# One activation table set for Ln and Exp, adjacent Gelus in each band, and a 3x3 convolution without two matrix blocks, in a four-layer convolution kernel

## The chip, the cores and the metric

The kernel runs on one core of one Trainium2 chip. The metric is the device time of one execution in microseconds (us). The time before is 4928.02 us, the median of three runs that lie between 4917.86 and 4933.94 us. One further execution was taken with the hardware profiler; all durations below come from it.

## What is computed

Four residual layers on x of shape (4, 384, 64, 64), float32, each on a group-normed input. Cut to what matters here:

```
x = x + attention(gn(x))       # layer 0: q,k,v from 96 channels, softmax over 4096 positions, 1x1 projection of 384
x = x + L1(gn(x))              # layer 1: 1x1 conv, 8x8 patch FFT filter, depthwise 3x3, gate, 1x1 conv:
                               #   x1, x2 = halves of the depthwise output (192 channels each); gelu(x1) * x2
x = x + L2(gn(x))              # layer 2: y3 = bn(depthwise 3x3(x)); y5 = bn(depthwise 5x5(x));
                               #   tok = bn(kw0*y3 + kw1*y5 + y1); gates; MLP 384 -> 768 -> 384 with bn and gelu
x = x + L3(gn(x))              # layer 3: depthwise 7x7, its kernel made from channel means and maxima
```

A norm needs 1/sqrt(var + eps). The kernel computes it on ScalarE as exp(-0.5 * ln(var + eps)).

## The kernel before

The program is written with a layer that records instructions, places tiles and orders each engine's queue by a priority heap over its own time estimates[...]. `tc.high_priority()` lifts the instructions of a block in that heap; `tc.issue_after(i)` puts them behind instruction i on i's engine.

**Stage A, 0 to about 2490 us (layers 0 and 1), `phase_a`.** Batches b = 0 to 3 go through `attention` (L739 on), 64 steps each. A step is four score matmuls (`sc_s`, L755, 32 rows each), two Exp activations of 128x1024 on ScalarE (`probs`, L763) and four value matmuls (`av`, L792). Beside the attention of batch b, `others` feeds pieces of other work: the statistics and the q, k, v of batch b+1 (`qkv`, whose `layer_norm` calls `rsqrt`, L354 and L355: one Ln and one Exp for each of eight blocks), and layer 1 of batch b-1. After about 2220 us the last batch's layer 1 runs alone.

Layer 1 works in 8 bands of 8 image rows. For each band `band_taps` (L967 to L997) accumulates nine taps for three tiles acc[0], acc[1], acc[2] on VectorE (L988; in the last batch some taps are matmuls). The channels are ordered so that acc[0] and the lower half of acc[2] are x1, and acc[1] and the upper half of acc[2] are x2. When acc[1] is done (j == 1), acc[0] goes through Gelu (L992) and is multiplied into acc[1] (L993); when acc[2] is done (j == 2), its lower half goes through Gelu into acc[0]'s upper half (L995), which is multiplied into acc[2] (L996). `band_out` (L1005, L1006) does the 1x1 convolution of the result some tiles later.

Ln, Exp and Gelu are table functions: where an activation's function is not in the active table set, the compiler puts an ACT_TABLE_LOAD ahead of it, which carries the line of that activation. Nothing in the kernel before chooses a set.

**Stage B, about 2490 to 3090 us (layer 2's depthwise convolutions), `phase_b`.** 12 units of 32 channels (four batches side by side on the partitions). A unit has 16 steps n, each for two channels. A step multiplies strips of the image (`z_`) with banded matrices (`toep`), which VectorE (even n) or GpSimd (odd n) makes from a row of taps and a band mask, one instruction of 128x1536 (`matrices53`, L1177). The taps come by DMA, a tile of 384 KB for four steps (`taps53`, L1163). `conv53` (L1196) runs, for each channel, three matmuls i of 256 columns over rows of the strip two apart: 128 columns for the 5x5 filter (v = 0), 128 for the 3x3 filter (v = 1), all into one bank `conv_m`. One ScalarE copy of 512 moves the bank into `d_o` (L1205), VectorE takes two statistics (L1208), and after each four steps two DMAs of 512 KB store d (L1211, ScalarE's queue). At a unit's end `conv_norms` makes its scales with one Ln and one Exp; in the next unit `unit_tok` reads d back (L1261, SyncE's queue, three buffers), combines it on ScalarE and VectorE (L1269, L1272, L1274, L1279) and stores tok (L1282). `unit_strips` loads and transposes a later unit's image (L1110, L1124).

**Stages E, F and G, 3125 to 4920 us:** layer 2's MLP (`phase_ef`: `h_s`, L1420; `h_m`, L1472) and layer 3 (`phase_g`: `conv_m`, L1786). There the change touches only which table set is active at a few places.

## Time and profile before

| | us |
|---|---|
| median of three runs | 4928.02 |
| the profiled execution's own time | 4921.93 |
| its span, first to last instruction | 4920.2 |
| PE busy | 4484.3 |
| DVE busy | 2787.8 |
| ACT busy | 2155.9 |
| POOL busy | 777.6 |

PE is TensorE's matmuls, PEld its weight loads, DVE is VectorE, ACT is ScalarE, POOL is GpSimd. Busy time is the union of an engine's instructions. A float32 matmul stands in the trace as two records, so counts of matmuls are twice those of the program. A group of instructions has a line, an engine, an operation and its tiles; behind its busy time stands the mean duration of one in ns and the time that the engine sat idle before them, with what ended it. The table loads have no tile.

### The profile page before, as it was taken

To read this page: it belongs to the slowest core of one execution; us is meant where nothing else is said; L and a number is where in the kernel's file an instruction comes from. 1 tells how busy PE (TensorE), PEld (TensorE's weight loads), DVE (VectorE), ACT (ScalarE), POOL (GpSimd) and SP (SyncE) were. 2 spreads that over 40 slices of the span, in tenths; PEclk is the share of its full clock that TensorE was granted. 3 is DMA by queue.
4 is the path that set the end of the run, shared out by engine and by line. 5 is a ranking of instruction groups with operands and counts; after the bars stand their busy time and mean duration, and the time that the engine had idled before them with its cause. 6 is when DMAs were issued, how large, how long until landed. Compare 5 with 4: busy or idle time off the path is not lost.

```text
span 4920.2 us, 47066 instructions
## 1 busy us (share of the span) xinstructions
PE 4484.3 (91%) x17289; PEld 2510.4 (51%) x17289; DVE 2787.8 (57%) x4506; ACT 2155.9 (44%) x2905; POOL 777.6 (16%) x593
## 2 busy tenths in 40 slices
PE   5999999999999999999978999699999997678988
PEld 2333444334443344435467888344444443577888
DVE  5322566645656345565867778555521113667898
ACT  5444444555445544445245666311123334753321
POOL 1000000000000000000035555000000001225554
PEclk9999999999999999999989999799999998788999
DMA  5210211111122111113259999776664444896776
GB/s 176 69 46 28 92 58 60 61 60 47 56 70 67 47 33 65 65 62 112 83 169 282 288 295 299 250 270 254 250 240 153 154 152 143 309 343 195 234 252 229
DMA packets 345844, 752.21 MB, mean 153 GB/s; under 512 B 22683, under 2 KB 172294, under 8 KB 336646
## 3 DMA queue, kind: packets, MB, share of 16 engines
q1 hardware_dynamic: 279864, 475.07, 31.4%
q0 software_dynamic: 32640, 151.28, 7.9%
q10 hardware_dynamic: 33102, 122.77, 6.4%
q8 instruction: 140, 2.29, 0.2%
q14 instruction: 98, 0.80, 0.1%
HBM read 446.76 MB, written 302.25 MB: 152 GB/s over the span
## 4 chain that ended last, share of the span: by engine, by line
PE 67%; DVE 13%; ACT 8%; DMA 7%; issue 4%; POOL 1%; SPq 0%; ACTq 0%; DVEq 0%; POOLq 0%
PE av L792 14%; PE h_s L1420 10%; PE h_m L1472 9%; PE conv_m L1196 9%; PE sc_s L755 5%; PE proj_m L825 4%; PE t_m L911 3%; DVE acc L988 3%; PE out_m L1006 2%; PE conv_m L1786 2%; PE out_m L1005 2%; PE back_m L936 2%; DMA wmix<-in_mix_t 1%; ACT probs L763 1%; DMA g_h<-h 1%
## 5 line engine op out<-in xcount | busy, mean ns | idle before, releaser
L792 PE MATMUL av<-probs,vt 128*128 128x512 f32 x2048 | 964.6, 606 | 0.1
L763 ACT ACTIVATE probs<-sc_s 128x1024 f32<-128x1024 f32 x512 | 501.1, 1021 | 721.3 <-PE av L792 717.9
L792 PEld LDWEIGHTS av<-probs,vt 128*128 128x128 f32 x2048 | 369.7, 192 | 467.9 <-issue 460.5
L1196 PE MATMUL conv_m<-toep,z 128*128 128x256 f32 x2304 | 520.1, 385 | 10.3 <-DVE toep L1177 6.4
L988 DVE SCALAR_TENSOR_TENSOR acc<-band,vecs,acc 128x512 f32<-128x512 f32 x708 | 496.6, 746 | 45.7 <-POOL band L949 40.0
L1472 PE MATMUL h_m<-f_h,cm_w_t 128*128 128x512 f32 x1152 | 496.6, 594 | 8.8 <-ACT f_h L1462 8.7
L1196 PEld LDWEIGHTS conv_m<-toep,z 128*128 128x128 f32 x2304 | 439.0, 193 | 71.7 <-DVE z L1129 4.9
L1786 PE MATMUL conv_m<-toep,z 128*128 128x128 f32 x3072 | 391.4, 285 | 40.5 <-POOL toep L1773 21.6
L1786 PEld LDWEIGHTS conv_m<-toep,z 128*128 128x128 f32 x3072 | 377.0, 201 | 42.8 <-POOL toep L1773 22.0
L1177 POOL TENSOR_TENSOR toep<-w,band 128x1536 f32<-128x1536 f32 x94 | 323.8, 3445 | 281.7 <-PE conv_m L1196 240.8
L1420 PE MATMUL h_s<-e_tok,cm_w_t 128*128 128x512 f32 x768 | 362.6, 594 | 5.5 <-DMA e_tok<-tok 5.5
L1472 PEld LDWEIGHTS h_m<-f_h,cm_w_t 128*128 128x128 f32 x1152 | 219.3, 191 | 286.1 <-issue 273.5
L755 PE MATMUL sc_s<-q,k 32*128 32x512 f32 x2048 | 296.5, 648 | 25.7 <-ACT probs L763 25.2
L1480 DVE BATCH_NORM_STATS2 h_st<-f_h 128x6 f32<-128x512 f32 x96 | 66.4, 694 | 429.2 <-ACT f_h L1479 429.2
L911 PE MATMUL t_m<-w_in_t,xb 128*128 128x384 f32 x768 | 276.4, 494 | 4.7 <-DVE coef L928 3.5
L825 PE MATMUL proj_m<-xm,w_proj_t 128*128 128x512 f32 x576 | 269.4, 606 | 9.4 <-DVE xm L778 6.5
L1427 ACT COPY e_h<-h_s 128x1024 f32<-128x1024 f32 x96 | 97.2, 1012 | 400.8 <-PE h_s L1420 400.8
L832 DVE SCALAR_TENSOR_TENSOR x_res<-proj_m,bn_c,x_res 128x512 f32<-128x512 f32 x96 | 71.7, 747 | 308.7 <-PE proj_m L825 308.7
L1420 PEld LDWEIGHTS h_s<-e_tok,cm_w_t 128*128 128x128 f32 x768 | 146.5, 191 | 189.7 <-issue 183.6
L1429 DVE BATCH_NORM_STATS2 h_st<-e_h 128x6 f32<-128x512 f32 x192 | 123.5, 685 | 199.5 <-ACT e_h L1427 199.5
L911 PEld LDWEIGHTS t_m<-w_in_t,xb 128*128 128x128 f32 x768 | 142.3, 191 | 141.0 <-issue 58.0
L1420 PE MATMUL h_s<-z,cm_w_t 128*128 128x512 f32 x384 | 196.1, 592 | 0.0
(392 smaller groups left out, 6119.3 us busy)
## 6 DMA issues: line engine op xcount, KB each, us to landing
d<-d_o ACTq DMA_DIRECT2D x96, 512.0 KB
c_d<-d SPq DMA_DIRECT2D x96, 512.0 KB
hid<-e_h ACTq DMA_DIRECT2D x16, 3072.0 KB
f_h<-hid SPq DMA_DIRECT2D x16, 3072.0 KB
x_in<-in_x SPq DMA_DIRECT2D x96, 256.0 KB
x_res<-in_x SPq DMA_DIRECT2D x32, 768.0 KB
xa<-x_res POOLq DMA_DIRECT2D x32, 768.0 KB, 3.9
xa_in<-xa SPq DMA_DIRECT2D x32, 768.0 KB
```

Of the source, the lines that this page charges most:

```text
L755: nc.tensor.matmul(s[:, g], lhsT=k4[32 * g : 32 * g + 32, c], rhs=q[i][32 * g : 32 * g + 32], start=True, stop=True,)
L763: nc.scalar.activation(p[:, h * 1024 : (h + 1) * 1024], s[:, 2 * h : 2 * h + 2].rearrange("p a b -> p (a b)"), AF.Exp, scale=0.25,)
L792: nc.tensor.matmul(av, lhsT=vt[:, 4 * c + v, :], rhs=p[:, v * 512 : (v + 1) * 512], start=c == 0 and v == 0, stop=c == 7 and v == 3,)
L825: nc.tensor.matmul(m, lhsT=self.w_proj[:, j, o * P : (o + 1) * P], rhs=xm[:, j], start=j == 0, stop=j == NJ - 1,)
L911: nc.tensor.matmul(m[:, 0:C], lhsT=xb[:, j], rhs=self.w_in[:, j, :], start=j == 0, stop=j == NJ - 1,)
L988: nc.vector.scalar_tensor_tensor(out, src(j, k), w, done, ALU.mult, ALU.add)
L1177: eng.tensor_tensor(t, self.w53[:, at : at + 192].rearrange("p (m n) -> p m n", n=8).unsqueeze(2).to_broadcast([P, 24, 8, 8]), band.rearra ...
L1196: nc.tensor.matmul(m[:, c * 256 : (c + 1) * 256], lhsT=self.z_[:, at : at + P], rhs=t[:, 12 * c + 4 * i : 12 * c + 4 * i + 4].rearrange("p ...
L1420: nc.tensor.matmul(s[:, v, :], lhsT=w1[:, j, o * P : (o + 1) * P], rhs=t[j][:, v * 512 : (v + 1) * 512], start=j == 0, stop=j == NJ - 1,)
L1429: nc.vector.bn_stats(st[:, o, 8 * b + 2 * i + v, :], h[:, o, v * 512 : (v + 1) * 512])
L1472: nc.tensor.matmul(m, lhsT=w2[:, o, j * P : (j + 1) * P], rhs=h[:, o, v * 512 : (v + 1) * 512], start=o == 0, stop=o == 5,)
L1786: nc.tensor.matmul(m[:, ch * P : (ch + 1) * P], lhsT=self.z_[:, at : at + P], rhs=t[:, 8 * c + 2 * i : 8 * c + 2 * i + 2].rearrange("p m a ...
```

## The change

1. `ln_exp` loads the set natural_log_exp_and_others, in which both Ln and Exp lie. It is called at the start, and behind each use of another function (Gelu, Sigmoid, Sqrt) on ScalarE.
2. In `band_taps` both Gelus of a band move to j == 2 and stand next to each other with high priority: first that of acc[2]'s lower half, into a tile of its own (`gelu`, one buffer), then that of acc[0], then `ln_exp`; both multiplications follow.
3. In layer 2 each group of 8 rows of a filter's matrix is a block of 64 columns. `_pair` orders a channel's blocks so that the two blocks of the 3x3 filter that its taps don't reach are left out: 10 blocks for a channel in place of 12. The middle matmul (i = 1) goes first with 256 columns, i = 0 and i = 2 have 192 and write the bank's first and last 192 columns. The matrices and taps shrink from 24 to 20 blocks a step (128x1280 and 320 KB), and the copy out of the bank becomes two copies of 256 (5x5: the middle 128 columns of each channel; 3x3: its first and last 64).
4. In `nets` the two Sigmoids for k3 and k5 stand ahead of those of the gate.

```diff
 def _pair(u, v):
-    return np.stack([u, v], axis=4)
+    u, v = (t.reshape(*t.shape[:4], 2, 8) for t in (u, v))
+    blocks = [
+        (v, 0, 0), (u, 0, 0), (u, 0, 1),
+        (v, 1, 0), (u, 1, 0), (u, 1, 1), (v, 1, 1),
+        (u, 2, 0), (u, 2, 1), (v, 2, 1),
+    ]
+    return np.ascontiguousarray(np.stack([t[:, :, :, k, f] for t, k, f in blocks], axis=3))
...
+    def ln_exp(self, behind=None):
+        load = lambda: self.nc.scalar.preload_act_table_set("natural_log_exp_and_others")
+        if behind is None:
+            load()
+        else:
+            with self.tc.high_priority(), self.tc.issue_after(behind.ins):
+                load()
...
-            if j == 1:
-                nc.scalar.activation(acc[0], acc[0], AF.Gelu)
+            if j == 2:
+                g = self.wk("gelu", "gelu", 1)
+                with self.tc.high_priority():
+                    first = nc.scalar.activation(g[64:P], acc[2][0:64], AF.Gelu)
+                    with self.tc.issue_after(first.ins):
+                        last = nc.scalar.activation(acc[0], acc[0], AF.Gelu)
+                    self.ln_exp(last)
                 nc.vector.tensor_mul(acc[1], acc[1], acc[0])
-            if j == 2:
-                nc.scalar.activation(acc[0][64:P], acc[2][0:64], AF.Gelu)
-                nc.vector.tensor_mul(acc[2][64:P], acc[2][64:P], acc[0][64:P])
+                nc.vector.tensor_mul(acc[2][64:P], acc[2][64:P], g[64:P])
...
-        t = self.bt_p.tile([P, 24, 8, 8], F32, tag="toep", name="toep53", bufs=4)
-        at = n % 4 * 192
+        t = self.bt_p.tile([P, 20, 8, 8], F32, tag="toep", name="toep53", bufs=4)
+        at = n % 4 * 160
...
-            for i in range(3):
+            for i, k0, k1, to in ((1, 3, 7, 0), (0, 0, 3, 0), (2, 7, 10, 64)):
                 at = (c0 + c) * 132 + 4 * i
                 nc.tensor.matmul(
-                    m[:, c * 256 : (c + 1) * 256],
+                    m[:, c * 256 + to : c * 256 + to + 64 * (k1 - k0)],
                     lhsT=self.z_[:, at : at + P],
-                    rhs=t[:, 12 * c + 4 * i : 12 * c + 4 * i + 4].rearrange("p m a n -> p (m a n)"),
-                    start=i == 0,
+                    rhs=t[:, 10 * c + k0 : 10 * c + k1].rearrange("p m a n -> p (m a n)"),
+                    start=i == 1,
                     stop=i == 2,
                 )
-        mv = m.rearrange("p (c v n) -> p v c n", c=2, v=2)
+        mv = m.rearrange("p (c n) -> p c n", c=2)
         at = 2 * (n % 4)
-        nc.scalar.copy(self.d_o[:, :, at : at + 2], mv)
+        nc.scalar.copy(self.d_o[:, 0, at : at + 2], mv[:, :, 64:192])
+        ends = mv.rearrange("p c (k n) -> p c k n", n=64)[:, :, 0:4:3]
+        nc.scalar.copy(self.d_o[:, 1, at : at + 2].rearrange("p c (f n) -> p c f n", f=2), ends)
...
```

`ln_exp` is also called without an argument at the start of `phase_a` and behind `score_shifts`, and behind: the activation in `bn_of_four`, the last Sigmoid of the gate in `nets`, the gates' Sigmoids and the last Gelu of the MLP in `phase_ef`, and the Sqrt in `phase_g`.

More of the change, by code (lines that the diff above doesn't have):

```diff
@@ L392, in bn_of_four @@
         a, c = self.bn_scale_shift(name, mv[:, 0:1], mv[:, 1:2], g, b)
-        nc.scalar.activation(out, z, func, bias=c, scale=a)
+        self.ln_exp(nc.scalar.activation(out, z, func, bias=c, scale=a))
     def of_groups(self, name, v):
@@ L490, in phase_a @@
             self.open_psum(ctx, 2)
+            self.ln_exp()
             cp = ctx.enter_context(tc.tile_pool(name="a_const", bufs=1))
@@ L512, in phase_a @@
             self.score_shifts(cp)
+            self.ln_exp()
             self.w_proj = self.weight(cp, "w_proj_t")
@@ L1160, in taps53 @@
         if n < 16 * UNITS:
-            self.w53_ahead = self.bt_p.tile([P, 8 * 96], F32, tag="w53", name="w53")
+            self.w53_ahead = self.bt_p.tile([P, 8 * 80], F32, tag="w53", name="w53")
             src = self.ins["c53_t"][n // 64][:, n % 64 * 2 : n % 64 * 2 + 8]
-            self.nc.sync.dma_start(self.w53_ahead, src.rearrange("p c t n v -> p (c t n v)"))
+            self.nc.sync.dma_start(self.w53_ahead, src.rearrange("p c m n -> p (c m n)"))
     def matrices53(self, n):
@@ L1178, in matrices53 @@
             t,
-            self.w53[:, at : at + 192].rearrange("p (m n) -> p m n", n=8).unsqueeze(2).to_broadcast([P, 24, 8, 8]),
-            band.rearrange("p (a n) -> p a n", n=8).unsqueeze(1).to_broadcast([P, 24, 8, 8]),
+            self.w53[:, at : at + 160].rearrange("p (m n) -> p m n", n=8).unsqueeze(2).to_broadcast([P, 20, 8, 8]),
+            band.rearrange("p (a n) -> p a n", n=8).unsqueeze(1).to_broadcast([P, 20, 8, 8]),
             ALU.mult,
@@ L1320, in nets @@
         nc.tensor.matmul(m[:, B : 2 * B], lhsT=net[:, P : 2 * P], rhs=z2, start=True, stop=True)
-        self.gate = self.keep.tile([P, B], F32, tag="gate", name="gate")
-        nc.scalar.activation(self.gate, m[:, 0:B], AF.Sigmoid)
-        nc.vector.tensor_scalar(self.gate, self.gate, 0.5, None, ALU.subtract)
-        nc.scalar.activation(self.gate, self.gate, AF.Sigmoid)
         self.k3 = self.keep.tile([P, B], F32, tag="k3", name="k3")
@@ L1328, in nets @@
         nc.scalar.activation(self.k5, m[:, B : 2 * B], AF.Sigmoid, scale=-1.0)
+        self.gate = self.keep.tile([P, B], F32, tag="gate", name="gate")
+        nc.scalar.activation(self.gate, m[:, 0:B], AF.Sigmoid)
+        nc.vector.tensor_scalar(self.gate, self.gate, 0.5, None, ALU.subtract)
+        self.ln_exp(nc.scalar.activation(self.gate, self.gate, AF.Sigmoid))
         own = self.sm([P, B], "k_own")
@@ L1378, in phase_ef @@
                 gates = self.sm([P, B], "gates")
-                nc.scalar.activation(gates, z[:, j], AF.Sigmoid, bias=gc[:, j : j + 1], scale=ga[:, j : j + 1])
+                last = nc.scalar.activation(
+                    gates, z[:, j], AF.Sigmoid, bias=gc[:, j : j + 1], scale=ga[:, j : j + 1]
+                )
                 nc.vector.tensor_scalar(self.at[:, j, :], gates, a[:, j : j + 1], None, ALU.mult)
                 nc.vector.tensor_scalar(self.ct[:, j, :], gates, c[:, j : j + 1], None, ALU.mult)
+            self.ln_exp(last)
             stay = self.sm([P, B], "stay")
@@ L1461, in phase_ef @@
                     for o in range(6):
-                        nc.scalar.activation(
+                        last = nc.scalar.activation(
                             h[:, o, :], h[:, o, :], AF.Gelu, bias=c1[:, o : o + 1], scale=a1[:, o : o + 1]
                         )
+                    if b == B - 1 and i == 3:
+                        self.ln_exp(last)
                     if b == B - 1 and 0 < i:
@@ L1531, in phase_g @@
             nc.vector.tensor_reduce(self.mix2, sq, AX.X, ALU.add)
-            nc.scalar.activation(self.mix2, self.mix2, AF.Sqrt)
+            self.ln_exp(nc.scalar.activation(self.mix2, self.mix2, AF.Sqrt))
             for k in ("a_s", "b_s"):
```

## The prediction

> **What bounds the kernel now.** I read the page first, then the busy time by stage, ScalarE's groups, TensorE's waits, and stage B unit by unit. From the page:

> ```profile
> span 4920.2 us, 47066 instructions
> PE 4484.3 (91%) x17289; PEld 2510.4 (51%) x17289; DVE 2787.8 (57%) x4506; ACT 2155.9 (44%) x2905; POOL 777.6 (16%) x593
> PE   5999999999999999999978999699999997678988
> DMA  5210211111122111113259999776664444896776
> PE 67%; DVE 13%; ACT 8%; DMA 7%; issue 4%; POOL 1%; SPq 0%; ACTq 0%; DVEq 0%; POOLq 0%
> ```

> TensorE carries the kernel nearly everywhere. The one place where a second resource is also full is slices 21 to 25, stage B, where DMA reads 9 beside PE. The stretches by stage (each engine's busy us, granted clock, DMA share, GB/s):

> ```profile
> core 0: us, PE busy (x) PEld busy (x) DVE busy (x) ACT busy (x) POOL busy (x), PEclk, DMA share, GB/s
> 110.00:500.00 390.00, 375.73 (x1215) 149.55 (x1214) 117.73 (x177) 181.79 (x204) 8.44 (x14) 0.97 0.15 49
> 500.00:2220.00 1720.00, 1654.58 (x5423) 714.37 (x5423) 979.19 (x1661) 813.58 (x995) 65.14 (x126) 0.99 0.18 60
> 2490.00:3125.00 635.00, 568.95 (x2720) 492.51 (x2720) 470.45 (x923) 372.53 (x576) 323.81 (x94) 0.95 0.91 272
> ```

> In stage A ScalarE is about half idle and PE has only 65 us of idle time in 1720, so work taken off ScalarE pays only where PE waited for it. The table loads, among ScalarE's groups:

> ```profile
> L354 ACT ACT_TABLE_LOAD x66 | 84.7, 1283 | 21.2 <-POOL mean L1042 9.7 <-PE ln_v L642 4.1 <-DMA vecs<-in_vecs 3.4
> L355 ACT ACT_TABLE_LOAD x56 | 71.8, 1283 | 2.1 <-DMA w_proj_t<-in_w_proj_t 1.2
> L763 ACT ACT_TABLE_LOAD x46 | 59.0, 1283 | 0.8
> L992 ACT ACT_TABLE_LOAD x25 | 32.1, 1283 | 0.5
> L995 ACT ACT_TABLE_LOAD x19 | 24.4, 1283 | 5.7 <-DVE acc L988 5.4
> ```

> With seven single ones that is 219 loads, 281 us of ScalarE. What PE waited for from ScalarE between 500 and 2220 us:

> ```profile
> PE sc_s L755 <- ACT probs L763: 14.2, 22, 2.0
> PE v_m L685 <- ACT ln_rs L354: 9.5, 6, 2.7
> PE back_m L936 <- ACT t_t L919: 5.5, 5, 1.5
> ```

> With two smaller rows (3.2 and 0.8) 33.2 us; the same view of 0 to 500 us has 11.0, 4.2, 2.2 and 1.0, 18.4 us. So 52 us is about all that stage A can give. Stage B by units (1, 2, 5, 6 and 11; a unit starts with its first conv_m matmul):

> ```profile
> 2554.90:2598.60 43.70, 43.70 (x199) 38.34 (x199) 33.64 (x62) 24.18 (x36) 24.15 (x7) 0.96 0.96 265
> 2598.60:2652.80 54.20, 45.33 (x205) 38.84 (x204) 36.54 (x76) 28.40 (x44) 29.35 (x9) 0.97 0.93 281
> 2755.20:2803.40 48.20, 46.79 (x235) 40.97 (x235) 38.58 (x74) 30.65 (x48) 27.56 (x8) 1.00 1.00 291
> 2803.40:2851.60 48.20, 46.83 (x234) 40.85 (x234) 38.36 (x74) 30.47 (x48) 27.55 (x8) 1.00 0.99 298
> 3046.20:3088.80 42.60, 42.56 (x200) 37.25 (x200) 35.16 (x72) 22.51 (x38) 20.67 (x6) 1.00 0.91 283
> ```

> A steady unit is PE-bound (46.8 of 48.2 us) and has DMA at 0.99 to 1.00 at the same time. In unit 2 PE is not the limit: the chain of waits runs for 10.8 us through a c_d load there.

> [...] between 2855.59 and 2858.43 us two loads and a Ln of 0.24 us follow each other without a gap. I count 1.283 us. [...] 78 records of 256 columns in 16.94 us, 217 ns each, and 40 of layer 3's 128 columns in 4.47 us, 112 ns. [...]

> **The change part by part.**

> *Table loads, stage A.* In the order of the changed program's instructions 80 loads are left: two for each of 32 bands and 16 others. Stage A has 173 before (21 to 110 us, 20 to 500, 126 to 2220, 6 after) and 66 after; outside the bands none is left in the attention. Most of the ScalarE waits above end after a run that holds a load; I count three quarters. Before 500 us nearly all loads go: 0.75 x 18.4 = 14 us. From 500 to 2220 us loads go from 126 to 48, 62%: 0.62 x 0.75 x 33.2 = 15 us. Bounds: 0 to 52. The other 107 - (29 / 1.283 = 23) loads lie beside matmuls; taken away they give nothing, as ScalarE then waits longer for PE (L763 already waits 717.9 us for av).

> *Gelus, stage A.* 64 activations as before (631 and 627 ns). Queued behind the first Gelu on ScalarE are a t_t or band copy and the next two Exps; they now wait for VectorE once a band (acc[2]) and no longer also at acc[0] (L992 waited 22.3 us in all, L995 44.5). In the program's order the first Gelu stands as far behind its last tap as L995 did: one VectorE and one ScalarE instruction between. The multiplications come later by one Gelu (0.63 us) and a load; out_m hides that, as it stands tiles later, except at the batches' ends (out_m waited 10.0 us in two places for L996). Four ends x 1.9 us = 8 at most; I take 1. The extra buffer moves no DMA. Stage A: 14 + 15 - 1 = 28 us.

> *Convolution, stage B.* Of a unit's 192 records 64 stay at 217 ns and 128 go to 192 columns, halfway between 112 and 217: 164.5 ns. 128 x 52.5 ns = 6.7 us a unit, 81 us in 12. Weight loads stay, and layer 3's 112 ns shows that they fit below 164. ScalarE: 512-wide copies take 584 ns, 384-wide ones (L919, L939) 476 to 498, so 256-wide about 380: 2 x 380 - 584 = 176 ns x 16 = 2.8 us more a unit, less two loads, 2.6: nothing, at 31 of 48 us busy. toep on VectorE 1745 to 1455 ns, x 8 = 2.3 us less a unit; on GpSimd 3445 to 2870. DMA: 4 tap tiles a unit lose 64 KB each, 0.26 MB of 48.2 us x 295 GB/s = 14.2 MB: 1.8%, all on SyncE's queue, no issue more or less.
> So PE alone would allow 41.5 us for a steady unit. If the share of 1.00 is a ceiling, DMA allows 47. But the same share of 0.96 came with 265 GB/s in unit 1 and 298 at 0.99 in unit 6, so [...] the share isn't a hard wall. I take 44.5, the middle: 3.7 us x 7 units (4 to 10) = 26. Units 2 and 3 wait for data, but lose the two loads ahead of their scales: 3 each. Unit 0 (DMA 0.46) gets 6, unit 1 2, unit 11 3. Sum 43; bounds 14 (the 1.8%, unit 0 and the loads) and 78.

> *The rest.* Unit 11's scales are on the path to the last tok: 2.6 us. At F's end Ln and Exp stand alone: 2.6. At E's start the DMA of tok covers seven loads; if that cover were gone, 9 us more. Layer 3's conv untouched. 5 us; bounds 0 and 12. The Sigmoids' order in nets costs nothing beside unit 0's matmuls.

> Sum: 28 + 43 + 5 = 76 us. 4921.93 - 76 = 4846 for an execution like the profiled one; that one lies 6.1 us below the median of 4928.02, so I forecast 4852. About 0.3%, 15 us, is what a measurement can tell from no change.

> **The rivals.** *DMA is the wall* (0.22): stage B gives 14. For: share 1.00, 15.2 MB in unit 2 took 54 us. Against: 298 GB/s in unit 6. 28 + 14 + 5 = 47, 4881 us. *PE alone decides in B* (0.20): 28 + 75 + 5 = 108, 4820 us; for it, VectorE waited for c_d only in unit 2 and at the end. *Loads were all hidden in A* (0.08): 0 + 43 + 5, 4880. *The changed order loses it* (0.06): 4925. *Slower* (0.08): the first Gelu, raised to high priority, holds ScalarE's queue until VectorE has acc[2]; the Exps behind it are late and sc_s waits. L995 waited up to 9.9 us once. To end over 15 us slower it must cost PE 91 us, 3.8 us in each of the 24 bands beside attention; today all of L995's waits there are 20 us. With 4 us, 4948 us.

> **How the numbers follow.** Likeliest (0.36): 4852. The range, 4795 to 4912, holds the forecast's bounds and the three faster rivals. Faster 0.36 + 0.22 + 0.20 + 0.08 = 0.86, within 0.3% 0.06, slower 0.08.

> **What would show it.** Right: 80 table loads; PE's ScalarE waits in stage A at 20 us or so; conv_m records at 164 ns with a unit of 44 to 45 us, DMA still at 1.00 at over 305 GB/s, and new waits of VectorE's tok_m for c_d. Units of 47 us mean the DMA wall, of 42 PE alone. Wrong: stage A no shorter, or ScalarE waits for acc at L1011 above 90 us.

## The result, and the profile after

The changed kernel takes 4881.7 us (median of four runs, 4875.3 to 4895.4) where the kernel before, measured beside it, takes 4928.3: a ratio of 0.9914, with a 95% interval of 0.9895 to 0.9933. It is faster by 46.6 us. I forecast 76 and 4852 us; the result lies in the range, and on the number of the rival "DMA is the wall" (4881), but that is a coincidence, as the stages below show. The profiled execution took 4883.64 us. Its page:

```profile
span 4881.8 us, 47092 instructions
PE 4432.2 (91%) x17289; PEld 2492.5 (51%) x17289; DVE 2764.1 (57%) x4506; ACT 1988.4 (41%) x2958; POOL 728.7 (15%) x593
PE   5999999999999999989978889699999997778888
PEclk9999999999999999999979999899999998788999
DMA  5211212121211111113259999766664444896776
PE 31%; DVE 6%; DMA 6%; ACT 3%; issue 2%; POOL 1%; SPq 0%; ACTq 0%; DVEq 0%; POOLq 0%
```

ScalarE's busy time fell by 167.5 us: 139 loads less (219 - 80) of 1.283 us are 178, and the second copy of each bank takes some of it back. TensorE's fell by 52. The table loads and the convolution's new forms, among the groups (busy us, mean ns of one; behind the bar the idle time before them):

```profile
L339 ACT ACT_TABLE_LOAD x41 | 52.6, 1283 | 1.4 <-PEq L1928 0.7
L1011 ACT ACT_TABLE_LOAD x32 | 41.1, 1283 | 33.6 <-DVE acc L1005 33.0
L1216 PE MATMUL conv_m<-toep,z 128*128 128x192 f32 x1536 | 326.0, 336 | 0.0
L1225 ACT COPY d_o<-conv_m 128x256 f32<-128x256 f32 x192 | 71.5, 372 | 121.9 <-PE conv_m L1216 119.3 <-DMA c_d<-d 1.9 <-DMA z<-tok 0.4
```

No load stands any more at the lines of Ln and Exp (L369, L370 and L780; 66, 56 and 46 before), and the 64 Gelus have 32, one a band. A matmul's record lasts 336 ns, but the records overlap; 82 that follow each other in the chain of waits take 14.83 us, 181 ns each, and (217 + 2 x 164.5) / 3 is 182: the price of 164 ns was right. The stages (engines' busy us, granted clock, DMA share, GB/s), in the windows of before except that stage B ends earlier:

```profile
core 0: us, PE busy (x) PEld busy (x) DVE busy (x) ACT busy (x) POOL busy (x), PEclk, DMA share, GB/s
110.00:500.00 390.00, 385.19 (x1254) 153.78 (x1255) 122.64 (x182) 158.85 (x187) 8.62 (x14) 0.98 0.16 51
500.00:2220.00 1720.00, 1654.74 (x5409) 716.40 (x5408) 981.50 (x1687) 716.65 (x934) 65.89 (x127) 0.98 0.18 62
2485.00:3060.00 575.00, 504.54 (x2688) 466.37 (x2687) 427.04 (x871) 333.35 (x717) 272.26 (x94) 0.92 0.92 277
```

The landmarks of the two traces say where the 38.4 us between the spans came from (the medians are 46.6 us apart, since the profiled execution of before was faster than its median and that of after slower):

| stretch | before | after | gain | forecast |
|---|---|---|---|---|
| start to the last av of batch 0 | 512.0 | 490.1 | 21.9 | 14 |
| to the last av of batch 3 | 1688.8 | 1679.5 | 9.3 | 15 |
| last batch's layer 1, alone, to the first conv_m of B | 297.2 | 315.2 | -18.0 | -1 |
| stage B, first to last conv_m | 590.8 | 571.3 | 19.5 | 43 |
| from there to the end | 1831.4 | 1825.7 | 5.7 | 5 |

Two rows miss: layer 1 alone is 18 us longer, and stage B gave less than half. The units of B (4, 5, 6, 8 and 11; the last rows of before to compare are 48.20 us, with the clock at 1.00):

```profile
2675.30:2722.60 47.30, 41.28 (x236) 38.33 (x236) 37.04 (x73) 29.23 (x62) 23.19 (x8) 0.96 0.98 303
2722.60:2773.70 51.10, 44.52 (x237) 40.97 (x236) 36.73 (x73) 29.36 (x62) 23.22 (x8) 0.90 0.92 274
2773.70:2828.40 54.70, 45.26 (x240) 41.94 (x239) 38.86 (x80) 30.24 (x64) 23.13 (x8) 0.87 0.91 268
2877.80:2925.40 47.60, 44.13 (x235) 40.71 (x236) 35.18 (x69) 28.55 (x62) 23.16 (x8) 0.92 0.91 276
3020.80:3056.10 35.30, 35.26 (x197) 33.23 (x197) 32.70 (x71) 21.31 (x51) 17.40 (x6) 1.00 1.00 315
```

The last unit has no strips to make and is 7 us shorter than before; the best of units 4 to 10 have the 47 to 48 us that I had called the sign of the DMA wall. But a column to the left of DMA has changed too: the granted clock is no longer 1.00. It is the column I had not used.

### The profile page after: what moved, and what is told of

Read it like the earlier page. It is cut to its first block, busy times and chain, and to the rows that moved or that the text cites. A ratio compares the mean times of both kernels' runs of the same rounds, so it can differ in the third digit from the quotient of the medians.

```text
span 4881.8 us, 47092 instructions
## 1 busy us (share of the span) xinstructions
PE 4432.2 (91%) x17289; PEld 2492.5 (51%) x17289; DVE 2764.1 (57%) x4506; ACT 1988.4 (41%) x2958; POOL 728.7 (15%) x593
## 5 line engine op out<-in xcount | busy, mean ns | idle before, releaser
L780 ACT ACTIVATE probs<-sc_s 128x1024 f32<-128x1024 f32 x512 | 497.8, 1020 | 785.4 <-PE av L809 784.7
L1216 PE MATMUL conv_m<-toep,z 128*128 128x192 f32 (+1 forms) x2304 | 447.7, 356 | 17.7 <-DVE toep L1197 17.6
L1216 PEld LDWEIGHTS conv_m<-toep,z 128*128 128x128 f32 x2304 | 411.1, 198 | 40.7 <-issue 10.2
L1813 PEld LDWEIGHTS conv_m<-toep,z 128*128 128x128 f32 x3072 | 380.7, 203 | 40.5 <-POOL toep L1800 20.2
L1197 POOL TENSOR_TENSOR toep<-w,band 128x1280 f32<-128x1280 f32 x94 | 272.3, 2901 | 314.3 <-PE conv_m L1216 199.9
L772 PE MATMUL sc_s<-q,k 32*128 32x512 f32 x2048 | 294.9, 645 | 10.6 <-ACT probs L780 10.1
## 6 DMA issues: line engine op xcount, KB each, us to landing
d<-d_o ACTq DMA_DIRECT2D x96, 512.0 KB
c_d<-d SPq DMA_DIRECT2D x96, 512.0 KB
```

The costliest lines, as they stand in the source:

```text
L772: nc.tensor.matmul(s[:, g], lhsT=k4[32 * g : 32 * g + 32, c], rhs=q[i][32 * g : 32 * g + 32], start=True, stop=True,)
L780: nc.scalar.activation(p[:, h * 1024 : (h + 1) * 1024], s[:, 2 * h : 2 * h + 2].rearrange("p a b -> p (a b)"), AF.Exp, scale=0.25,)
L1197: eng.tensor_tensor(t, self.w53[:, at : at + 160].rearrange("p (m n) -> p m n", n=8).unsqueeze(2).to_broadcast([P, 20, 8, 8]), band.rearra ...
L1216: nc.tensor.matmul(m[:, c * 256 + to : c * 256 + to + 64 * (k1 - k0)], lhsT=self.z_[:, at : at + P], rhs=t[:, 10 * c + k0 : 10 * c + k1].r ...
L1813: nc.tensor.matmul(m[:, ch * P : (ch + 1) * P], lhsT=self.z_[:, at : at + P], rhs=t[:, 8 * c + 2 * i : 8 * c + 2 * i + 2].rearrange("p m a ...
```

## The experiments

Times are medians; the kernel before, measured beside them, took 4925.5 to 4927.3 us. Lengths of stages are from one profiled execution of each kernel. Kernels with the changed kernel's stage A put the last av between 2166.8 and 2174.1 us, and three with its stage B give that stage 571.3 to 576.1 us, so a difference of under some 5 us between two traces says little.

**The two halves of the change alone.** First the convolution without the rest: no `ln_exp`, Gelus and Sigmoids as before.

> The kernel before with the convolution's edit alone (blocks left out, 192-column matmuls, two copies). Stage B, first to last conv_m matmul, was 590.8 us before and is 571.3 after. If the conv's gain is limited by what feeds it and not by the other edits: 570 to 580 us, the rest of the kernel as before, total 20 us less (ratio 0.996). If the absence of the scales' table loads is what made B shorter: B at 585 us or more. If the full gain of the matmuls comes through once ScalarE keeps its old table loads and order: 515 us.

4917.0 us, ratio 0.998 [0.9973, 0.9987]; stage B 583.9 us, 6.9 shorter: between the first two expectations, and far from the full gain. Then the table set, the Gelus and the Sigmoids, with the convolution of before.

> The changed kernel with the convolution of before: table set, adjacent Gelus, Sigmoid order. Theory: attention ends (last av) at 2170 us in place of 2201, layer 1 of the last batch takes 315 us from there to the first conv_m in place of 297, stage B about 588 (its own loads gone), total 20 to 25 us less, ratio 0.995. Rival, the slower last layer 1 in the changed kernel was an accident of that build's instruction order: 297 to 303 us, total 35 us less.

4892.6 us, ratio 0.9929 [0.9906, 0.9951]; the last av at 2167.0, layer 1 alone 312.9 us, stage B 581.9. The stretch of layer 1 came as the theory had it; the gain of 34 us is above its 20 to 25. The halves give 10 and 34 us, together 44 of the 46.6, so they hardly disturb each other. The convolution, whose matmuls lost 81 us, earns 10. And this half alone shortens B by 9, the number that I had for the loads (3 for each of units 2, 3 and 11), but not there: units 2, 3 and 11 take 52.6, 53.6 and 42.6 us for 54.2, 52.5 and 42.6. It is unit 0 that became shorter, 48.7 us for 56.9. Before the change TensorE stopped in it for 4.0 us (net_m for net_z2s, the small network of `nets`; 7 loads of 1283 ns stand between 2490 and 2560 us, at L354, L355, L393 and L1322), and the clock there was 0.91; now this stop is gone and the clock is 1.00.

**Layer 1 alone, with its Gelus back.** In the last batch:

```diff
-            if j == 2:
+            if alone and j == 1:
+                nc.scalar.activation(acc[0], acc[0], AF.Gelu)
+                nc.vector.tensor_mul(acc[1], acc[1], acc[0])
+            elif alone and j == 2:
+                last = nc.scalar.activation(acc[0][64:P], acc[2][0:64], AF.Gelu)
+                if h == 7:
+                    self.ln_exp(last)
+                nc.vector.tensor_mul(acc[2][64:P], acc[2][64:P], acc[0][64:P])
+            elif j == 2:
```

> The changed kernel, but in the last batch, whose layer 1 runs beside nothing, each Gelu stands where it stood before (acc[0] at j == 1, acc[2] at j == 2, one table load for all bands). Theory, the pair at the band's end is what cost 18 us there (PE waits at out_m for acc): last av to first conv_m 297 us, total 18 us below the changed kernel, about 4864, ratio 0.987. Rival, that stretch grew for another reason (more ScalarE copies of strips in it, the order of statistics): 310 to 318 us and total as the changed kernel.

4873.6 us, ratio 0.9895 [0.987, 0.992]; the stretch takes 300.6 us, 14.6 less than after the change and 3.4 more than before it. The whole kernel is 8 us faster, not 18, and its interval overlaps that of the changed kernel. TensorE's waits for `acc` in it, first after the change, then with the Gelus back:

```profile
PE out_m L1025 <- DVE acc L1015: 18.8, 4, 9.8
```

```profile
PE out_m L1033 <- DVE acc L1023: 9.8, 1, 9.8
PE out_m L1034 <- DVE acc L1015: 3.3, 1, 3.3
```

Only 5.7 of the 14.6 us stand in these rows; the rest is spread, since each band's last products come later (the first `out_m` of the last batch 97.4 us after the last av, 85.4 before the change). The granted clock differs too: TensorE stood at 0.50 for 68.3 us of this stretch after the change, for 55.1 before it, and for 54.6 with the Gelus back. The edit also takes away 15 of the 18 loads that the changed kernel has in this stretch (7 before), so position and loads are not told apart.

**Both Gelus at their old places in all bands**, with `ln_exp` behind each (in the last batch only behind the last band's second): the table set without the adjacency.

> The changed kernel with the two Gelus of every band at their old places (acc[0] at j = 1, acc[2]'s half at j = 2), and the table set put back behind each (in the last batch only behind the last band's second). 34 more table loads stand beside the attention than in the changed kernel, 24 bands x 1.28 us = 31 us of ScalarE. Theory 'ScalarE has room beside the attention, adjacency buys nothing there': the last av of batch 3 at 2165 to 2175 (2169.6 with the Gelus adjacent), the stretch of layer 1 alone 298 to 302 us (315.2), time 4868 to 4875. Rival 'each load beside the attention costs TensorE about what it lasts, as the Exps behind it come late': the last av at 2190 or later, time 4890 or more.

4863.0 us, ratio 0.9861 [0.9842, 0.988], below the changed kernel's interval. Layer 1 alone takes 297.5 us, and the last av of batch 3 stands at 2166.2 us, although 96 loads stand ahead of it instead of 48. The theory's numbers for the attention and the stretch came out. So the adjacency, which saves those loads, earns nothing beside the attention; where the attention is gone, the pair with its two loads a band costs 18 us. ScalarE has the room: before the change it was busy for 813.6 of the 1720 us.

**Fewer bytes in stage B.** The load of the 3x3 result is left out of `unit_tok`, and the 5x5 result stands in for it, first in the changed kernel:

```diff
-            for v, d in enumerate((d5, d3)):
+            for v, d in enumerate((d5,)):
...
-                nc.vector.scalar_tensor_tensor(m, d3[:, part], s[:, 1:2], m, ALU.mult, ALU.add)
+                nc.vector.scalar_tensor_tensor(m, d5[:, part], s[:, 1:2], m, ALU.mult, ALU.add)
```

> The changed kernel without the load of the 3x3 result in unit_tok: the 5x5 result stands in for it, so that 2.1 MB of a unit's 13.9 MB of DMA are left out and all instructions on the engines stay. Theory DMA wall: a unit's period follows the bytes, 48.5 us on average of units 4 to 10 in the changed kernel to 42 or 43, first to last conv_m 571 to 510 or 515 us. Rival, the order of the queues (TensorE waits at strip_m for unit_x's activation behind the bank copies on ScalarE): units stay at 47 us or more and the waits at strip_m stay at 25 us or so. Both: 44 to 46 us.

4834.5 us, ratio 0.9811 [0.9783, 0.9838]; stage B 532.5 us, units 4 to 10 between 43.2 and 46.6: the third expectation, that bytes and order both count. The same cut in the kernel before:

> The kernel before, without the load of the 3x3 convolution's result in unit_tok (the 5x5 result stands in for it in the combination): 25 MB less to read in stage B, all else as it was. It is the control of the same cut in the changed kernel, which took 39 us from B. Theory 'TensorE set the steady units before': units 4 to 10, 48 us with 46.8 of it matmuls, stay within 1 us, only the units that waited for data (2, 3 and the last) are shorter, B falls by 10 to 18 us; so the cut is worth more than twice as much after the change as before it. Rival 'the DMA engines already set the pace before': units 4 to 10 fall to 46 or less and B falls by 25 to 40 us, as after the change.

4898.6 us, ratio 0.9937 [0.9914, 0.9959]; stage B 567.9 us, 22.9 less. A steady unit of it:

```profile
2785.60:2833.10 47.50, 46.26 (x234) 40.74 (x235) 38.68 (x74) 30.47 (x48) 27.59 (x9) 1.00 0.82 257
```

DMA fell from a share of 1.00 to 0.82 and the unit from 48.2 to 47.5: before the change TensorE set the steady unit, although the DMA engines looked full. The stage as a whole lost more than the 10 to 18 us of the theory, most of it in units 2 and 3. After the change the same cut is worth 39 us of B instead of 23 (less than the twice that I expected), so bytes do weigh more, but a unit of 45 us without them is not the 41.5 that I estimated for TensorE's work alone.

**The order at a unit's end.** TensorE's largest new wait in B is strip_m for `unit_x` (26.0 us in the view of its waits, 1.8 before). I moved the transposes one step behind their activation:

```diff
+        for n in range(8):
+            i, h = n // 4, n % 4
+            if j and n:
+                turn((n - 1) // 4, (n - 1) % 4)
...
+            if j and n == 7:
+                turn(1, 3)
```

> The changed kernel, with the transposes of unit_strips one step behind the activation of their piece (in step n those of piece n-1, in the last step two), so that TensorE no longer comes to them while ScalarE is still busy with the two d_o copies and the activation. Theory 'the order of ScalarE's queue': TensorE's waits of strip_m for unit_x fall from 27.8 us to under 8, and stage B (571 us) ends at 545 to 555, units 4 to 10 at 46; time 4857 to 4865. Rival 'the DMA engines': their share was already 0.90 to 1.00 in these units, so the waits only move to tok_m and conv_m (for matrices whose taps come late), and B stays at 565 to 572; time 4876 to 4882.

4872.1 us, ratio 0.9878 [0.985, 0.9906]. Stage B is shorter, 559.8 us, between the two expectations, but not for the reason given: the wait is still 23.8 us. The planner keeps both activations of a half image together behind the unit's last copies. What went are the 51.1 and 54.7 us of units 5 and 6, now 44.8 and 46.9. In the changed kernel the chain of waits went through a late c_d at the end of unit 6 (in unit 5 no wait for c_d stands in the trace):

```profile
2815.38 0.39 ACT d_o L1227
2815.76 0.26 SPq L1283
...
2816.07 8.77 DMA c_d<-d
...
2824.94 0.77 DVE tok_m L1294
```

**Four buffers for c_d** in the changed kernel (`bufs=3` to `bufs=4` in the pool of c_d), to ask whether such loads are late for want of a free buffer.

> The changed kernel with four buffers for c_d in place of three (the matrices and taps that became smaller leave the room); nothing else differs, and no byte less is moved. In the changed kernel's trace between 2803 and 2815 us hardly a c_d packet moves, DMA stands at 203 GB/s, and the c_d load that tok_m waits for is issued only at 2815.76 and lands 8.8 us later. Theory 'c_d loads come late because their buffers come free late': VectorE's waits of tok_m for c_d fall from 14.9 us to under 5, stage B from 571 to 550 to 560 us, time 4862 to 4872. Rival 'the rate of the DMA engines, whose share is 0.90 to 1.00 already': B 566 to 575 us and 4877 to 4886, the waits as before or moved to other loads.

4880.6 us, ratio 0.991 [0.9895, 0.9926]; B 572.9 us, tok_m's wait 14.3 us for 14.9. The buffer is not it; the numbers are those of the rival, which has the rate of the DMA engines behind these waits.

**The corrections together.** The last batch's Gelus back and late transposes:

> Both corrections in the changed kernel: the Gelus of the last batch's layer 1 (which runs alone) at their old places, and the transposes of unit_strips one step late. If they add: 8 us from the first (as measured, 4873.6) and what the late transposes give by themselves. Theory 'the order of ScalarE's queue': 4849 to 4858. Rival 'the DMA engines': 4868 to 4874, the first correction alone.

4859.5 us, ratio 0.9858 [0.9838, 0.9877]: 22 us below the changed kernel, near the first theory's span and far from the second's. All Gelus at their old places, and late transposes:

> The changed kernel with the Gelus of every band at their old places and the set put back behind each (as in the run that took 4863.0 us), and with the transposes of unit_strips one step late (stage B 559.8 us for 571.3 by itself, though TensorE's waits for unit_x hardly fell). If the two are independent: 4863.0 - 10 = 4853, 4849 to 4857. Rival 'the shorter B of the late transposes was an accident of that kernel's order, and comes and goes with whatever stands ahead of it': 4860 to 4866.

4850.0 us, ratio 0.9852 [0.9839, 0.9864]: these two are independent, as expected. With the fourth buffer besides:

> All three corrections together: Gelus at their old places with the set put back behind each, late transposes, four buffers for c_d. If buffers and late transposes mend different waits: 4838 to 4848. If they mend the same one (DVE's late c_d) or the DMA rate stands behind both: 4850 to 4857, no better than without the fourth buffer.

4846.2 us, ratio 0.9843 [0.983, 0.9856], inside the span expected if the buffer mends a wait of its own, but with an interval that overlaps that of the run above. It is the fastest of the kernels that still do all loads, 36 us below the changed kernel.

**What the units of these kernels show.** Four units of the kernel that took 4850.0 us (7 to 10), which all run the same instructions in the same order and all end with the same stop of 2.7 us for `unit_x`:

```profile
2796.60:2844.60 48.00, 44.38 (x236) 40.96 (x236) 36.37 (x74) 29.13 (x62) 23.18 (x8) 0.91 0.94 285
2844.60:2891.50 46.90, 41.93 (x236) 38.70 (x236) 36.76 (x75) 29.02 (x62) 23.16 (x8) 0.95 1.01 305
2891.50:2940.00 48.50, 44.45 (x236) 40.97 (x236) 36.59 (x75) 29.13 (x62) 23.18 (x8) 0.90 0.94 282
2940.00:2984.70 44.70, 40.38 (x235) 37.35 (x236) 36.70 (x75) 29.03 (x62) 23.16 (x8) 1.00 0.98 308
```

Where the granted clock is 1.00, the unit takes 44.7 us, with DMA at 0.98 and 308 GB/s: the unit I forecast. Where the clock is 0.90 it takes 48.5, with DMA at 0.94 and 282 GB/s. The 3.8 us between the two stand in TensorE's busy time (44.45 against 40.38), not in its waits. (A unit's row begins at its first conv_m, after the clock has fallen behind the stop ahead of it; the periods below begin at that stop.) The stop itself, in steps of 2 us, in the kernel that took 4846.2 us:

```profile
2880.00:2882.00 2.00, 0.44 (x3) 0.14 (x1) 1.24 (x4) 0.82 (x3) 2.00 (x1) 1.00 0.92 263
2882.00:2884.00 2.00, 0.88 (x4) 0.88 (x5) 2.00 (x2) 2.00 (x2) 2.00 (x2) 0.64 0.73 204
2884.00:2886.00 2.00, 1.92 (x10) 1.52 (x9) 0.43 (x1) 1.70 (x4) 1.00 (x1) 0.50 1.05 403
...
2890.00:2892.00 2.00, 2.00 (x7) 1.82 (x7) 0.41 (x1) 0.61 (x1) 0.00 (x0) 0.50 0.79 226
2892.00:2894.00 2.00, 2.00 (x13) 1.86 (x11) 0.60 (x1) 0.60 (x2) 0.00 (x0) 0.80 1.17 274
```

The time at 0.50 in stage B, added up from the trace's record of the clock (stretches that begin in B; an earlier one reaches 2.9 us into B before the change, and 4.9 us into it in the last row, the experiment below):

| kernel | stage B | at half clock in B |
|---|---|---|
| before | 590.8 | 20.5 |
| before, without the 3x3 load | 567.9 | 13.7 |
| tables and Gelus alone | 581.9 | 20.5 |
| convolution alone | 583.9 | 105.8 |
| after | 571.3 | 92.2 |
| after, without the 3x3 load | 532.5 | 58.0 |
| late transposes, Gelus back in the last batch | 558.1 | 92.2 |
| all three corrections | 555.5 | 88.7 |
| the same, a load earlier | 560.6 | 54.6 |

It does not set the stage's length by itself: 92.2 us stand beside 571.3 and beside 558.1, and 54.6 beside 560.6.

The price comes from the four kernels with late transposes, whose units 5 to 10 have one order of TensorE's work and one stop for `unit_x` at the end (in units 3 and 4 the order differs a little). From a unit's last conv_m to the next unit's, the 32 periods by the time at half clock in them:

| at half clock in the period, us | periods | shortest, median, longest, us |
|---|---|---|
| 0 | 3 | 44.8, 45.7, 46.1 |
| 3.4 | 11 | 45.4, 46.1, 46.4 |
| 6.8 | 3 | 47.4, 47.4, 48.3 |
| 10.2 | 15 | 47.8, 48.4, 49.1 |

(48.4 - 46.1) / (10.2 - 3.4) = 0.34 us for each us at half clock. It is a rough price: units 5 to 10 alone give (48.4 - 45.5) / 6.8 = 0.43, a straight line through all 32 periods 0.32. That longer waits make both the longer unit and the half clock is not what the traces show: in units 5 to 10 TensorE's stops add up to 3.3 to 4.5 us in the periods with 10.2 us at half clock, and to 3.3 to 5.4 us in the others. The kernel before has the same effect with hardly a stop (1.4 us a unit): of its units 4 to 10 the five without half clock take 48.2 or 48.3 us, the two with 3.4 us of it 49.9, 0.5 us for each.

**Taking the stop away.** In the kernel of 4846.2 us the second half of a unit's image is loaded three pieces earlier, so that its activations come in mid-unit:

```diff
-            if h == 0:
+            if n in (0, 2):
+                k = (0, 2).index(n)
                 x = self.bx_p.tile([P, 2048], F32, tag="x", name="unit_x")
```

> The last kernel (4846.2 us, stage B 555.5) with one thing moved: the load of the second half of a unit's image is issued three pieces earlier (at piece 2, not with piece 4), so that its two activations no longer stand in ScalarE's queue behind the last d_o copies of a unit. In the last kernel TensorE idled 2.7 us there in units 7 to 10, and right after it the granted clock was 0.50 for 10.2 us in each; in stage B the clock was at 0.50 for 88.7 us in all (20.5 us before the change). Theory 'short idle of TensorE at the unit's end, then half clock': the stop at the unit's end goes, the time at 0.50 in B falls below 45 us, steady units take 44 to 45.5 us instead of 47.8, B 525 to 538 us, time 4817 to 4830. Rival 'the DMA engines hold 47 to 48 us a unit': the stop moves elsewhere (VectorE's tok_m waits longer for c_d, conv_m for its matrices), steady units 47 us or more, B 550 to 557, time 4842 to 4850.

4847.7 us, ratio 0.9842 [0.9828, 0.9855]: no change, and B takes 560.6 us. The theory's times failed, and the time and the steady unit are those of the rival (4842 to 4850, 47 us or more). The time at half clock in B fell from 88.7 to 54.6 us, but the stop did not go, it was replaced. A steady unit, and what TensorE waited for in it (us in total, times, longest):

```profile
2838.90:2886.60 47.70, 41.60 (x235) 38.97 (x235) 36.35 (x74) 28.78 (x63) 23.25 (x8) 0.96 0.98 292
```

```profile
PE cn_rep L1260 <- DVE st L1241: 3.4, 1, 3.4
PE strip_m L1134 <- ACT unit_x L1158: 2.2, 1, 2.2
PE conv_m L1227 <- ACT z L1141: 0.9, 2, 0.5
```

There are 6.5 us of stops where there were 3.3, and a half clock of 3.4 us in place of 10.2: the 3.2 us lost make up for the 6.8 x 0.34 = 2.3 won, and more. No DMA transfer stands in the chain of waits from 2838 to 2888 us, which goes through ScalarE, VectorE and TensorE, so this trace does not show the rival's mechanism either. So this run neither removed the stop nor freed the unit; that a unit without any stop takes 44 us with this DMA load has not been shown by an edit, only by the units above in which the same stop brought no half clock.

## Why the prediction was right or wrong

*Table loads.* Right in number (80) and price (1283 ns). (Before the change stage A has 172 loads, not 173: one lies across the edge of two of my windows.) Before 500 us I took three quarters of 18.4 us and got 14; batch 0 ended 21.9 us earlier, 6.2 of them ahead of the first av, where 12 loads stood and now 2 do. Of ScalarE's waits ahead of 500 us 2.4 are left of 18.4. From 500 to 2220 us the mechanism was smaller than I had it: the sign I named, 20 us for the whole of stage A, failed, since 30.2 of 33.2 us are left there. With the 4.8 of ln_v and the one for VectorE between them, they are:

```profile
PE back_m L953 <- ACT t_t L936: 15.3, 9, 2.1
PE out_m L1025 <- DVE acc L1015: 12.6, 2, 9.8
PE sc_s L772 <- ACT probs L780: 10.1, 10, 1.8
```

sc_s fell from 14.2 to 10.1 and the 9.5 us of v_m are gone, but back_m rose from 5.5 to 15.3: another tile of ScalarE's queue is late now. out_m, for the later products, has 12.6 for 10.0, but 9.8 and 8.2 of these stand behind the last av, in the stretch where layer 1 is alone. Batches 1 to 3 gave 9.3 us for 15. That the two add up to 31.2 for 29 is luck: one is too small by about as much as the other is too large.

*Gelus.* The step that failed first. I priced the later products at 1 us, with a bound of 8, as something that happens at batches' ends. In the last batch nothing lies beside the bands, so the whole stretch follows them: 18 us, of which 14.6 and 17.7 came back with the two runs that put the Gelus back. Whether the place of the Gelus or the two loads that came with them costs it, no run tells apart. The cover that I named, "tiles later", is the attention's, and there it held: the run with the Gelus apart has the same last av. The rival "slower" had the mechanism nearest to it, but priced it for the bands beside the attention, where it cost nothing. Its sign stayed away: ScalarE's waits for acc at L1011 are 58.4 us, not 90.

*Convolution.* The term of the sum that was mis-sized: 3.7 us for each of units 4 to 10, 26 in all. The steady units gave nothing (340.9 us before, 345.4 after). The matmul price was right, the copies (372 and 376 ns for 380) and toep (2901 ns on GpSimd for 2870) too, and units of 44.7 and 44.8 us exist. What I left out is that TensorE stops in a shorter unit, above all at its end, and the clock behind it: the stops add up to 6.4 to 6.7 us in each of units 4 to 8 and to 4.0 and 4.3 us in units 9 and 10, for 1.4 us a unit before. Time at half clock in B rose by 71.7 us; at 0.34 that is 24, and 43 - 24 = 19 against the 19.5 measured. Much of that fit is luck: the price lies anywhere from 0.32 to 0.43, units 5 and 6 lost 14 us that they do not lose with late transposes (the late c_d is seen at the end of one of them), and unit 11, forecast to gain 3, gained 7.3. That stop and clock cause the loss is argued from units of one order; no edit took the stop away.

*DMA is the wall.* Its total came out by luck (B gave 19.5 for its 14, and layer 1 alone lost 18 that it did not have), its mechanism in the long units did not: the units of 51.1 and 54.7 us moved 274 and 268 GB/s at a share of 0.92 and 0.91, where units of 44.7 and 35.3 us moved 308 and 315: the long ones waited, they were not full. It is not free of bytes either: without the 3x3 load B lost 39 us, of which 34 us less of half clock explain 12. How the other 27 divide between the rate and the lateness of single loads is open. So DMA stays a part of the cause whose size is not known. "PE alone" (42 us a unit) was seen in no steady unit that has all its loads; and the ground I gave for it was a misreading, as VectorE waited for c_d in units 6, 9 and 10 before the change too (5.1 us in three waits; 14.9 us in five after it, the new waits that I had named as a sign).

*The rest*, 5 us: 5.7.

## What to carry to other kernels

When matmuls are made shorter, look for the place where TensorE may then stop, and read the granted clock there: here units 5 to 10 of the kernels with late transposes, of one order of work and one stop for `unit_x`, had a median of 48.4 us with 10.2 us at half clock, and of 45.5 with 3.4. A full DMA column beside it was, before the change, only a neighbour: with 0.82 in place of 1.00 the steady unit took 47.5 us for 48.2. An edit that is hidden beside other work has to be priced again for the stretch in which that work is missing; here two adjacent Gelus with their loads bought nothing where they were hidden and cost 18 us where they were not. A planner that moves instructions can answer a local correction with another stop, as in the last experiment, so the next trace has to show that the stop is gone, and not just that it has moved.

## What was not expected of the hardware

- In the kernels with late transposes, with nearly the same order of TensorE's work in all units, a unit took 44.8 to 46.4 us where the clock was at 0.50 for 3.4 us or not at all, and 47.8 to 49.1 us where it was for 10.2. Why the same stop of 2.7 us, in four units of the kernel of 4850.0 us, came with the one or the other was not shown. Of the 38 falls of the clock behind 2000 us in the kernel of 4850.0 us, 36 followed a step of 3.4 us with TensorE busy for half of it or less (35 of the 37 between 2000 and 4870 us in the changed kernel's trace); steps with 0.62 to 0.70 kept the full clock. It is no sharp limit: two falls followed steps with 0.58 and 0.80, and some steps with 0.41 to 0.57 kept the full clock.
- In the two last kernels the falls in the last steady units (from unit 8 on in one, from unit 6 on in the other) are 47.8 us apart, which is 14 steps of 3.41 us, with 10.2 us of half clock in one and 3.4 in the other, and the unit takes 47.7 to 47.8 us in both. Whether the one sets the other, no run tried.
- DMA's share is no measure of what is left: 0.98 stood for 292 GB/s in one unit and for 308 in another, and taking 18 points of it away changed a steady unit before the change by 0.7 us.
